# A relational graph layer with a highway gate: node order by one-hot matmuls, the last group's sums kept on chip, x + h kept in the output

## The chip, the cores and the metric

The kernel runs on one core of one Trainium2 chip. The metric is the device time of one execution in microseconds (us). Three timed runs of the kernel before gave 1312.29, 1313.91 and 1315.41 us; their median, 1313.91 us, is the number to be compared. The profile shows one further execution, taken by the hardware profiler.

## What is computed

There are N = 1250 nodes with D = 1024 features, R = 8 relations and E = 20000 edges (src, dst, type), all float32. Cut to what matters, the reference is:

```python
h = relu(layernorm(x))
u = h @ root + bias
for r in range(8):
    sums = segment_sum(h[src] * (type == r), dst)      # a sum over edges
    cnt  = segment_sum(type == r, dst)
    u += (sums / max(cnt, 1)) @ weight[r]
z = concat([u, h]) @ w_gate + b_gate
out = x + tanh(u) * z + h * (1 - z)
```

## The kernel before

**Order of the matrix products.** The kernel multiplies first and sums over edges afterwards: it forms h @ weight[r] for all nodes, and each edge then fetches one row of that product. Eleven matrices are multiplied, one stage each: the eight weights are stages 0 to 7, root is stage 8, the lower half of w_gate (which meets h) is stage 9, called LAST, and the upper half (which meets u) is the gate at the end, stage 10. Every product uses a scheme with seven smaller products in place of eight. Stages 1 to 9 run as seven kinds each, written (stage, kind); `kind` (L284) issues a kind as five calls, numbered 0 to 4, and at each call a hook `between` lets other work be written into the instruction streams. In most kinds the product is split a second time: sums of quarters are made on VectorE (DVE; L264 to L274), TensorE (PE) multiplies (L309), ScalarE (ACT) copies sums in PSUM (L401, L424), and DVE adds in PSUM (L415, L436). PE waits for L401 and L415 inside the kind. In "regular" kinds (L228) the second split is left out. Stage 0 and the gate work in five pairs of node blocks, by `product` (L549, matmuls at L564). There are ten blocks of 128 nodes, the last with 98.

**The order is written out by hand.** Each engine runs its own instructions strictly in the order in which the program writes them. PE, DVE, ACT, GpSimd (POOL) and SyncE (SP) are all scheduled in this way, and a semaphore wait holds back all that stands behind it on its engine. Indirect DMAs (gathers and scatters by a list of row numbers) are issued by POOL, plain ones by SP.

**The index.** Edges are put into a table by destination and group: relations 0 to 4 are group 0, relations 5 to 7 group 1. `to_table` (L813) scatters the 157 columns of edges, 4 bytes each, and follows each scatter with three small memsets on POOL (L823). `order` (L1051) then counts the edges of each node, and ranks the nodes of a group by that count: for each of ten columns a comparison with all 1280 nodes (L838) gives `pos`, the place of each node. `rows_and_weights` (L750) turns places into a list: ten scatters of 128 numbers of 4 bytes to DRAM (L753), one load of the list (L763), `node_key` on POOL (L766), and ten gathers of table rows into `idx` (L705). This is done once per group. `any_over` (L1361) with `largest` (L1343) then asks, by two transposes on PE, whether any node has more edges than the table holds, and `counts` and `weights` make the factors `rcp` and `w_of` in the kinds that follow. At the mark `BEGIN` = (5, 2) the sums over edges may start; one kind ahead of it all engines branch on `n_any` (L1519).

**The sums over edges.** Since nodes are ranked, block d of group g needs at most K[g][d] slots: 118 in group 0, 75 in group 1. A slot (`add_slot`, L1241) is one gather on POOL of 128 rows of 4 KB (L1244) into one of five buffers `got`, and one multiply-add on DVE into the block's sum `u` (L1249). `edges` (L1267) makes a list of steps, one slot each, with the loads and stores of `u` between them, and `spread` (L1302) deals these steps out over the calls of the kinds named to it, by the weights `SHARE`. Group 0 starts its sums from the bias and is dealt over the kinds (5, 2) to (7, 6); its sums are scattered to `u_dram` by node (L711). All engines then branch on `n_pass` (L1568). Group 1 is dealt over the kinds (8, 0) to (9, 5). It starts from gathers of `u_dram` and works blocks 4 to 9 first, then 0 to 3. Blocks 4 to 9 are written to `last_dram` (L1601). To blocks 1 to 3 the product with root is added by an accumulating gather from `hr_dram` (an indirect DMA that adds to what is in its target), to the others by a plain gather into `got` and an addition on DVE (L1608). Sums `u` live in a pool of four buffers.

**The gate.** For each pair i of blocks, seven calls j: `gate_load` brings u of pair i+2 back from `last_dram`; `gate_h` gathers h rows into `got` and takes tanh(u) on ACT (L1683); `gate_turned` transposes u on PE; `gate_less` makes tanh(u) - h on DVE (L1698); `gate_rows` gathers x + h from `xh_dram` and the h part of z by an accumulating gather on top of the bias, multiplies by tanh(u) - h and adds x + h (L1664, L1665). `finish` (L1751) multiplies each quarter of the product by tanh(u) - h and adds the rest, and the finished rows are scattered to `out` (L711). The rows of the last block leave in three pieces (`scatter_piece`, L1636). x + h was written to `xh_dram` by `with_x` (L909) in stages 0 and 1.

Of the kernel before, what the change touches and what calls it, by code (L numbers as in the profile page):

```python
# [21 lines left out]
def tile_rgcn_highway(  # L22
# [53 lines left out]
    BEGIN = (5, 2)  # L76
# [3 lines left out]
    ENDS = 5  # L80
# [36 lines left out]
    xh_dram = dram.tile([N, D], F32, name="xh_dram")  # L117
    last_dram = dram.tile([N, D], F32, name="last_dram")
# [7 lines left out]
    node_dram = [dram.tile([KEYS, 1], I32, name=f"node_dram{g}") for g in range(G)]  # L126
# [567 lines left out]
    pos_i = const.tile([P, G, ND], I32, name="pos_i")  # L694
# [14 lines left out]
    def to_rows(of, frm, at, group):  # L709
        nc.gpsimd.memset(apart, 0.0)  # L710
        ins = nc.gpsimd.indirect_dma_start(  # L711
            out=of, out_offset=bass.IndirectOffsetOnAxis(ap=at, axis=0), in_=frm, in_offset=None)
        tc.declare_no_dep(ins.ins, query=no_wait, group=group, reason="rows differ")
        tc.add_to_no_dep_group(group, ins.ins)
# [35 lines left out]
    def rows_and_weights(g):  # L750

        for d in range(ND):
            ins = nc.gpsimd.indirect_dma_start(  # L753
                out=node_dram[g][:, :],
                out_offset=bass.IndirectOffsetOnAxis(ap=pos_i[:, g, d:d + 1], axis=0),
                in_=ids[:, d:d + 1], in_offset=None,
                bounds_check=KEYS - 1, oob_is_err=False)
            tc.declare_no_dep(ins.ins, query=no_wait, group="nodes", reason="places differ")
            tc.add_to_no_dep_group("nodes", ins.ins)
            if d % 2:  # L760
                yield
        yield
        nc.gpsimd.dma_start(node[:, g, :], node_dram[g].rearrange("(d p) o -> p (d o)", p=P))  # L763
        yield
        yield
        nc.gpsimd.tensor_single_scalar(node_key[:, g, :], node[:, g, :], g * KEYS, op=OP.add)  # L766
        for d in range(ND):
            rows_of(idx[:, g, d, :], table_rows, node_key[:, g, d:d + 1])
            if d % 2:
                yield  # L770
# [42 lines left out]
    def to_table(row_col, at_i, c):  # L813
# [8 lines left out]
        for _ in range(3):  # L822
            nc.gpsimd.memset(apart, 0.0)  # L823
# [17 lines left out]
    room_all = keep.tile([P, 4 * H + 4 * P], F32, name="inner")  # L841
    ys_room = [room_all[:, k * Q:(k + 1) * Q] for k in range(2)]
    with ExitStack() as early:
# [20 lines left out]
        class Normed:  # L864
# [186 lines left out]
        def order():  # L1051

            with tc.tile_pool(name="sort", bufs=1) as sp:
# [16 lines left out]
                for g in range(G):  # L1070
# [4 lines left out]
                    nc.vector.tensor_copy(pos_i[:, g, :], pos[:, g * ND:(g + 1) * ND])  # L1075
                    for _ in rows_and_weights(g):
                        pass
                for _ in range(3):
                    yield
# [132 lines left out]
    with ExitStack() as edges_part:  # L1212
# [40 lines left out]
        def new_u(d):  # L1253

            return upool.tile([P, D], F32, name="u")

        def first_u(g, d):

            n = nrows(d)
            u = new_u(d)  # L1260
# [6 lines left out]
        def edges(g, blocks, to, late=0, more={}):  # L1267
# [4 lines left out]
            nb = len(blocks)  # L1272
            starts = [late + sum(K[g][d] for d in blocks[:b]) for b in range(nb + 1)]
            leaves = [starts[b + 1] - 1 + GOT for b in range(nb)]
            reads = [max(-1, starts[b] - (9 if d in more else 5),
                         leaves[b - UB] if b >= UB else -1) for b, d in enumerate(blocks)]
            u, then = {}, {}
            for t in range(-1, leaves[-1] + 4):
                for b, d in enumerate(blocks):
                    if starts[b] <= t < starts[b + 1]:  # L1280
                        k = t - starts[b]
                        add_slot(u[d], g, d, k, idx[:, g], w_of[:, g])
                for b, d in enumerate(blocks):
                    if t == leaves[b]:
# [3 lines left out]
                for b, d in enumerate(blocks):  # L1288
                    if t == reads[b]:
                        u[d] = first_u(g, d)  # L1290
                    if d in more and t == starts[b] - 4:
# [10 lines left out]
        def spread(e, total, of):  # L1302

            share = [0 if s == LAST and n > ENDS else SHARE[n] for s, n in of]
            parts, said = CALLS * sum(share), [0, 0]

            def between(k):
                s, n, _ = at_call
                said[0] += 0 if s == LAST and n > ENDS else SHARE[n]
# [3 lines left out]
                if said[0] == parts:  # L1313
# [5 lines left out]
        def kinds(s, n, last):  # L1319

            return [(a, b) for a in range(s, last + 1) for b in range(7) if (a, b) >= (s, n)]
# [21 lines left out]
        def largest(*pairs):  # L1343
            p = sum_bank("ps_q")
            for k, (of, to) in enumerate(pairs):
                nc.tensor.transpose(p[:1, k * P:(k + 1) * P], of, ident)
            for k, (of, to) in enumerate(pairs):
                nc.vector.reduce_max(to, p[:1, k * P:(k + 1) * P], axis=AX.X)
        def whole(of, to, add, least):

            nc.vector.tensor_scalar(of, of, float(add), float(least), op0=OP.add, op1=OP.max)
            nc.vector.tensor_copy(to, of)

        def passes_over(*more):

            top = const.tile([1, 1], F32, name="top")
            largest((most[:, 0:1], top), *more)
            whole(top, n_over, MORE - SLOTS, 0.0)
            nc.vector.tensor_single_scalar(n_over, n_over, 2, op=OP.arith_shift_right)

        def any_over():  # L1361

            bad = const.tile([1, 1], F32, name="bad")
            passes_over((most[:, 2:3], bad))
            whole(bad, n_far, 0.0, 0.0)
            nc.vector.tensor_max(n_any, n_over, n_far)
        def beside(e, total, s, i, last):


            between = spread(e, total, kinds(s, i, last))  # L1370
            while s <= last:
                step(s, i, between)
                s, i = next(steps, (NM, 0))
# [7 lines left out]
        def beside_group():  # L1381

            yield
            while at_call[2] != 2:
                yield
            any_over()
            yield
            for g in range(G):
                yield from counts(g)
                yield  # L1390
# [94 lines left out]
        def order_again():  # L1485
# [13 lines left out]
            for g in range(G):  # L1499
# [8 lines left out]
                nc.vector.tensor_copy(pos_i[:, g, :], pos[:, g * ND:(g + 1) * ND])  # L1508
                for _ in rows_and_weights(g):
# [49 lines left out]
        first_group = with_ready(edges(0, range(ND), u_back(0), LATE))  # L1559
        next(first_group)  # L1560
        s, i = beside(first_group, sum(K[0]) + LATE + 1, s, i, R0[2] - 1)
# [35 lines left out]
        HELD = 4  # L1597

        def to_last(d, u):
            n = nrows(d)  # L1600
            nc.sync.dma_start(last_dram[d * P:d * P + n, :], u[:n])  # L1601
# [231 lines left out]
```

## Time and profile before

| | |
|---|---|
| median of three timed runs | 1313.91 us |
| the profiled execution | 1306.43 us |
| its span, first to last instruction | 1304.5 us |
| PE busy | 1266.7 us of the span |
| DVE busy | 978.2 us |
| POOL busy | 629.5 us |
| ACT busy | 252.1 us |
| DMA moved | 286.25 MB |
| slots, gather and multiply-add (L1244, L1249) | 193 |

How to read it: the profile is of one execution. Rows named by a source line group the instructions that this line issued. "Idle before, releaser" says how long the engine stood still ahead of an instruction and what ended that wait; "issue" means that the profile shows nothing the engine waited for, "remote" that a semaphore moved and no instruction in the profile is seen to have moved it. A view by windows gives the busy time of each engine in a stretch of the span, with the granted TensorE clock (1.00 is full speed), the mean busy share of the 16 DMA engines, and GB/s.

### The profile page before, as it was taken

The numbers are of one execution on the slowest core, as the hardware profiler recorded it, in microseconds if no ns is written. First come the engines' busy times: TensorE is split into PE (matmuls) and PEld (weight loads), VectorE is DVE, ScalarE is ACT, GpSimd is POOL, SyncE is SP. The second block draws the span as 40 slices with busy tenths as digits, with TensorE's granted clock in tenths as the row PEclk, the third lists the DMA queues.
The fourth block names the chain that finished last, engine by engine and source line by source line (L and its number), as shares of the span: only waits on it lengthen the run. The fifth ranks groups of instructions, "written<-read, shape, count | busy, mean of one in ns | idle before, by whom it ended". The sixth has DMA issues, their size and how long they took to land. (4 is left out here: it accounts for less than half of the span.)

```text
span 1304.5 us, 13959 instructions
## 1 busy us (share of the span) xinstructions
PE 1266.7 (97%) x4430; PEld 832.6 (64%) x4430; DVE 978.2 (75%) x1377; ACT 252.1 (19%) x462; POOL 629.5 (48%) x975
## 2 busy tenths in 40 slices
PE   9999999999999999799999999999899998999996
PEld 5444777777777777575767666675656655644443
DVE  7963576555454896666899999997889897757974
ACT  3452221221121121112102111210110021102210
POOL 0046666665663045411356665665376557305531
PEclk9999999999999999899999999999999998999999
DMA  8777244534634746453757989799589868949951
GB/s 307 249 222 196 94 154 155 205 126 145 211 118 149 245 98 151 110 191 106 244 189 245 324 305 383 269 330 339 183 308 341 331 193 264 315 153 287 324 158 61
DMA packets 126597, 286.25 MB, mean 219 GB/s; under 512 B 33733, under 2 KB 35362, under 8 KB 126386
## 3 DMA queue, kind: packets, MB, share of 16 engines
q1 hardware_dynamic: 81890, 164.96, 37.6%
q0 software_dynamic: 44336, 119.80, 28.7%
q8 instruction: 35, 0.57, 0.2%
q10 hardware_dynamic: 288, 0.52, 0.1%
q14 instruction: 48, 0.39, 0.1%
HBM read 217.52 MB, written 82.71 MB: 230 GB/s over the span
## 5 line engine op out<-in xcount | busy, mean ns | idle before, releaser
L309 PE MATMUL ps<-w,h_all 128*128 128x256 f32 (+1 forms) x1216 | 371.7, 454 | 9.0 <-issue 9.0
L1244 POOL DMA_INDIRECT got<-y,idx x193 | 262.2, 1359 | 233.5 <-DVE u L1249 134.3
L309 PEld LDWEIGHTS ps<-w,h_all 128*128 128x128 f32 x1216 | 231.9, 191 | 128.9 <-issue 105.3
L1249 DVE SCALAR_TENSOR_TENSOR u<-got,w_of,u 128x1024 f32<-128x1024 f32 (+1 forms) x193 | 247.1, 1283 | 34.3 <-DMA got<-y,idx 25.9
L815 POOL DMA_INDIRECT table<-row_col,at_i x157 | 166.1, 1058 | 171.3 <-issue 100.5
L316 PE MATMUL ps_b<-w,h_all 128*128 128x512 f32 x504 | 226.6, 592 | 0.6 <-PEq L1519 0.6
L309 PE MATMUL ps_n<-w,w 128*128 128x256 f32 x800 | 192.2, 383 | 13.1 <-DVE ps L415 11.2
L309 PEld LDWEIGHTS ps_n<-w,w 128*128 128x128 f32 x800 | 151.8, 191 | 59.3 <-DVE ps L415 17.8
L316 PEld LDWEIGHTS ps_b<-w,h_all 128*128 128x128 f32 x504 | 95.8, 190 | 94.8 <-issue 91.6
L564 PE MATMUL ps_b<-w,h_all 128*128 128x512 f32 x312 | 139.3, 593 | 1.0 <-ACT row L614 0.7
L564 PEld LDWEIGHTS ps_b<-w,h_all 128*128 128x128 f32 x312 | 58.6, 190 | 73.6 <-issue 70.1
L415 DVE TENSOR_TENSOR ps<-ps_n,inner 128x256 f32<-128x256 f32 x100 | 40.8, 428 | 80.4 <-PE ps L309 75.5
L309 PE MATMUL ps<-w,w 128*128 128x256 f32 x400 | 94.8, 380 | 0.0
L309 PE MATMUL ps_q<-w,w 128*128 128x256 f32 x400 | 94.6, 379 | 0.2 <-DMA w<-lefts_dram 0.2
L309 PE MATMUL ps_n<-w,h_all 128*128 128x256 f32 x400 | 94.5, 379 | 0.0
L424 ACT COPY ps<-ps_n 128x512 f32<-128x512 f32 x100 | 53.0, 574 | 193.9 <-PE ps_n L309 182.6
L401 ACT COPY ps<-ps_n 128x256 f32<-128x256 f32 x100 | 32.2, 360 | 280.9 <-PE ps_n L309 216.8
L309 PEld LDWEIGHTS ps_n<-w,h_all 128*128 128x128 f32 x400 | 76.1, 190 | 15.5 <-issue 5.7
L309 PEld LDWEIGHTS ps<-w,w 128*128 128x128 f32 x400 | 76.4, 191 | 10.5
L309 PEld LDWEIGHTS ps_q<-w,w 128*128 128x128 f32 x400 | 75.9, 190 | 11.0 <-DVE w L367 0.6
L224 DVE TENSOR_TENSOR w<-w,w 128x2048 f32<-128x2048 f32 x36 | 82.2, 2284 | 0.3
L823 POOL MEMSET apart<- 128x1 f32 x471 | 52.2, 111 | 18.1
(213 smaller groups left out, 1195.2 us busy)
## 6 DMA issues: line engine op xcount, KB each, us to landing
w<-in_L_gnn_weight_dram SPq DMA_DIRECT2D x31, 1024.0 KB
w<-lefts_dram SPq DMA_DIRECT2D x48, 512.0 KB
y<-row SPq DMA_DIRECT2D x84, 256.0 KB
y<-w SPq DMA_DIRECT2D x42, 256.0 KB
w<-in_L_gnn_w_gate_dram SPq DMA_DIRECT2D x8, 1024.0 KB
lefts_dram<-w SPq DMA_DIRECT2D x14, 512.0 KB
h_dram<-h_all SPq DMA_DIRECT2D x9, 512.0 KB
y<-row SPq DMA_DIRECT2D x9, 512.0 KB
```

The costliest lines, as they stand in the source:

```text
L224: nc.vector.tensor_sub(w[to], w[a], w[b])
L309: nc.tensor.matmul(p, a[:, k], b[:, k], start=(fresh and k == 0), stop=(k == a.shape[1] - 1), skip_group_check=True)
L316: nc.tensor.matmul(to, h_op[NP - 1][:, ORDER[n], k], w[:, k], start=(fresh and k == 0), stop=(k == KQ - 1), skip_group_check=True)
L401: nc.scalar.copy(banks[2 * u][:, :H], xs[u])
L415: nc.vector.tensor_add(banks[2 * u][:, H:], xs[u], ys[:, u * H:(u + 1) * H])
L424: nc.scalar.copy(banks[2 * u + 1].rearrange("p (a n) -> p a n", a=2), xs[u][:, None, :].to_broadcast([P, 2, H]))
L564: nc.tensor.matmul(b[:, at], aop[:, i, k, :], w.of[i][:, k, at], start=(fresh and k == 0), stop=(k == KQ - 1), skip_group_check=True)
L815: ins = nc.gpsimd.indirect_dma_start(out=table[:, :], out_offset=bass.IndirectOffsetOnAxis(ap=at_i[:, c:c + 1], axis=0), in_=row_col[:, c: ...
L823: nc.gpsimd.memset(apart, 0.0)
L1244: nc.gpsimd.indirect_dma_start(out=t[:n], out_offset=None, in_=y[g][:, :], in_offset=bass.IndirectOffsetOnAxis(ap=at[:n, d, k:k + 1], axis=0),
L1249: nc.vector.scalar_tensor_tensor(u[:n], t[:n], w, u[:n], op0=OP.mult, op1=OP.add)
```

## The change

1. **Node order** (`nodes_in_order` in place of `rows_and_weights`). The place of each node is split into its high part and its low 7 bits. DVE makes two one-hot tables from them (128 x 1280 and 128 x 200, bf16), ten matmuls of 128 x 20 on PE invert the order into a bank of PSUM, and DVE forms `node` and `node_key` from it. The matmuls stand at call 2 of a kind. The twenty scatters L753, the two loads L763 and `node_dram` are gone; the gathers of `idx` stay. `any_over` is moved from the kind after the index up to stage 1, between the scatters of edges.
2. **Where the sums stand.** `BEGIN` is (5, 1). Group 0 is dealt over (5, 1) to (8, 2) and its branch on `n_pass` stands ahead of (8, 3). Group 1 is dealt over (8, 3) to (9, 6) and, with the weight `GATE` = 6, over the first three pairs of the gate. Its blocks run in the order 0 to 9.
3. **The last group's sums stay on chip.** `last_dram`, its stores and `gate_load` are gone. The sums of blocks 4 to 8 lie in `h_all`, in the places of the first two left factors, which kinds (9, 0) and (9, 1) read last. The product with root is added by an accumulating gather for all ten blocks: for blocks 3 to 9 four steps ahead of their first slot, for blocks 0 to 2 after their last, from call 3 of (9, 0) on.
4. **The gate.** `with_x` stores x + h to `out`, and `xh_dram` is gone. tanh is taken of -u, and h is added to it by an accumulating gather. The h part of z is gathered one pair ahead. `finish` adds z to the product and then multiplies by -1 and by h - tanh(u), and the rows are added to `out` by accumulating scatters. `got` is no longer used for rows of hr, h and x + h.

```diff
-    BEGIN = (5, 2)
+    BEGIN = (5, 1)
+    CHANGE = (8, 3)
-    ENDS = 5
+    GATE = 6
+    U_LATER = range(4, 9)
+    HR_LATER = 3
...
-    def rows_and_weights(g):
-        for d in range(ND):
-            ins = nc.gpsimd.indirect_dma_start(
-                out=node_dram[g][:, :],
-                out_offset=bass.IndirectOffsetOnAxis(ap=pos_i[:, g, d:d + 1], axis=0),
-                in_=ids[:, d:d + 1], in_offset=None,
-                bounds_check=KEYS - 1, oob_is_err=False)
...
-        nc.gpsimd.dma_start(node[:, g, :], node_dram[g].rearrange("(d p) o -> p (d o)", p=P))
...
-        nc.gpsimd.tensor_single_scalar(node_key[:, g, :], node[:, g, :], g * KEYS, op=OP.add)
+    def nodes_in_order(g, pos, ids_f, a, b, small, now=False):
...
+        nc.vector.tensor_copy(hi_i, pos)
+        nc.vector.tensor_single_scalar(hi_i, hi_i, 7, op=OP.arith_shift_right)
+        nc.vector.tensor_copy(hi, hi_i)
+        nc.vector.scalar_tensor_tensor(lo, hi_i, float(-P), pos, op0=OP.mult, op1=OP.add)
+        nc.vector.tensor_tensor(a, lo[:, :, None].to_broadcast([P, ND, P]),
+                                many[:, None, :].to_broadcast([P, ND, P]), op=OP.is_equal)
+        nc.vector.tensor_tensor(b[:, :, :ND], hi[:, :, None].to_broadcast([P, ND, ND]),
+                                many[:, None, :ND].to_broadcast([P, ND, ND]), op=OP.is_equal)
+        nc.vector.tensor_tensor(b[:, :, ND:], b[:, :, :ND],
+                                block[:, :, None].to_broadcast([P, ND, ND]), op=OP.mult)
+        nc.vector.tensor_scalar(b[:, :, :ND], b[:, :, :ND], ids_f[:, :1], None, op0=OP.mult)
+        yield
+        while not now and at_call[2] != 2:
+            yield
+        p = sum_bank("ps_q")
+        for c in range(ND):
+            nc.tensor.matmul(p[:, :2 * ND], a[:, c], b[:, c], start=(c == 0), stop=(c == ND - 1))
+        nc.vector.tensor_copy(lo_f := small[:, P + 4 * ND:P + 5 * ND], p[:, :ND])
+        nc.vector.scalar_tensor_tensor(node[:, g, :], p[:, ND:2 * ND], float(P), lo_f,
+                                       op0=OP.mult, op1=OP.add)
+        nc.vector.tensor_single_scalar(node_key[:, g, :], node[:, g, :], g * KEYS, op=OP.add)
...
-                nc.sync.dma_start(xh_dram[self.d * P:self.d * P + n, :], to[:n])
+                nc.sync.dma_start(out[self.d * P:self.d * P + n, :], to[:n])
...
+            checks = [any_over]
             for c in range(NCH):
                 to_table(row_col, at_i, c)
                 if c % 3:
                     yield
+                    if checks and at_call[0] and at_call[2] == 2:
+                        checks.pop()()
...
+            if g == G - 1 and d in U_LATER:
+                return h_op[d - U_LATER[0]][:, :2].rearrange("p a k f -> p (a k f)")
             return upool.tile([P, D], F32, name="u")
...
-        s, i = beside(first_group, sum(K[0]) + LATE + 1, s, i, R0[2] - 1)
+        s, i = beside(first_group, sum(K[0]) + LATE + 1, s, i, CHANGE)
...
-            t = got()
-            rows_of(t[:n], hr_dram[:, :], node[:n, LG, d:d + 1])
-            us[d] = u
-            return lambda: nc.vector.tensor_add(u[:n], u[:n], t[:n])
+            rows_of(u[:n], hr_dram[:, :], node[:n, LG, d:d + 1], OP.add)
...
-                to_rows(out, t[:n], node[:n, LG, d:d + 1], "out")
+                to_rows(out, t[:n], node[:n, LG, d:d + 1], "out", OP.add)
...
-                hs[part] = got()
-                rows_of(hs[part][:n], h_dram[:, :], node[:n, LG, d:d + 1])
-                nc.scalar.activation(place_of("d", i, part)[:n], us[d][:n], AF.Tanh)
+                nc.scalar.activation(place_of("d", i, part)[:n], us[d][:n], AF.Tanh, scale=-1.0)
...
-                nc.vector.tensor_sub(dt[:n], dt[:n], hs[part][:n])
+                rows_of(place_of("d", i, part)[:n], h_dram[:, :], node[:n, LG, d:d + 1], OP.add)
...
-        between = spread(last, LATE + sum(K[LG]) + GOT + 4, kinds(s, i, LAST))
+        last = edges(LG, keep_u, LATE, {d: add_hr for d in range(HR_LATER, ND)}, 4, False)
+        between = spread(last, LATE + sum(K[LG]) + 8, kinds((s, i), (NM - 1, NP - 2)))
...
-                    nc.vector.tensor_mul(to, of[:n], place_of("d", i, part)[:n, at])
-                    nc.vector.tensor_add(to, to, place_of("z", i, part)[:n, at])
+                    nc.vector.tensor_add(to, of[:n], place_of("z", i, part)[:n, at])
...
+                    nc.vector.scalar_tensor_tensor(to, to, -1.0, place_of("d", i, part)[:n, at],
+                                                   op0=OP.mult, op1=OP.mult)
```

More of the change, by code (lines that the diff above doesn't have):

```diff
@@ L1074, in order @@
                         yield
[L1075 to L1079, printed above, removed]
+                    yield from nodes_in_order(g, pos[:, g * ND:(g + 1) * ND], ids_f, junk,
+                                              sp.tile([P, 2 * ND * ND], BF16, name="b"),
+                                              sp.tile([P, P + 5 * ND], F32, name="small"))
         HEAVY = True
@@ L1287, in edges @@
                     then[t]()
[L1288 to L1289 removed]
+                for d in blocks:
+                    if t == reads[d]:
                         u[d] = first_u(g, d)
[L1291 removed]
+                    if d in more and t == starts[d] - 4:
                         more[d](d, u[d])
@@ L1341, in passes_needed, with beside @@
             nc.vector.tensor_max(n_pass, n_over, beyond_i)
[L1343 to L1371, printed above, removed]
+        def beside(e, total, s, i, end):
+            between = spread(e, total, kinds((s, i), end))
+            while (s, i) != end:
                 step(s, i, between)
-                s, i = next(steps, (NM, 0))
+                s, i = next(steps)
             return s, i
```

194 lines of the change are left out of this document (92 added, 102 removed).

## The prediction

> **What bounds the kernel now.** I read the page first, then who PE waited for, then the engines by windows of 25 us, and the timeline where PE stood still.
>
> ```profile
> span 1304.5 us, 13959 instructions
> PE 1266.7 (97%) x4430; PEld 832.6 (64%) x4430; DVE 978.2 (75%) x1377; ACT 252.1 (19%) x462; POOL 629.5 (48%) x975
> PE ps_n L309 <- DVE ps L415: 11.2, 5, 5.6
> PE ps L309 <- issue: 9.0, 1, 9.0
> PE ps_n L309 <- ACT ps L401: 1.8, 4, 1.1
> PE ps_b L564 <- ACT row L614: 0.7, 1, 0.7
> ```
>
> PE is busy for 1266.7 of 1304.5 us, so 37.8 us are all that an edit can win on PE, and any instruction added to PE costs its length. The waits (total, times, longest, in us) name the stalls: 9.0 us once, with a releaser that the profile does not know, and 11.2 + 1.8 us where PE waited for DVE or, through ACT, mostly for DVE again. The windows show where. Columns: busy us and count of PE, PEld, DVE, ACT and POOL, then granted clock, DMA share and GB/s.
>
> ```profile
> 525.00:550.00 25.00, 18.23 (x69) 14.32 (x70) 12.98 (x29) 3.34 (x7) 8.59 (x10) 0.86 0.43 94
> 875.00:900.00 25.00, 23.93 (x78) 14.39 (x77) 24.83 (x35) 2.28 (x5) 12.69 (x13) 1.00 0.94 326
> 900.00:925.00 25.00, 22.59 (x83) 15.24 (x82) 18.08 (x23) 2.87 (x6) 9.69 (x9) 1.00 0.80 286
> 925.00:950.00 25.00, 23.69 (x82) 15.18 (x81) 17.88 (x25) 5.69 (x11) 13.83 (x10) 1.00 0.62 188
> 950.00:975.00 25.00, 23.60 (x81) 14.99 (x80) 22.13 (x22) 4.62 (x9) 17.61 (x13) 1.00 0.93 333
> 1000.00:1025.00 25.00, 25.00 (x73) 13.55 (x72) 24.54 (x30) 1.06 (x2) 15.73 (x12) 1.00 0.97 352
> 1075.00:1100.00 25.00, 19.45 (x68) 14.10 (x67) 19.97 (x20) 3.18 (x7) 19.22 (x14) 0.86 0.83 253
> 1200.00:1225.00 25.00, 25.00 (x71) 11.96 (x70) 24.45 (x30) 4.99 (x8) 16.54 (x15) 1.00 1.04 326
> 1275.00:1300.00 25.00, 19.15 (x52) 9.42 (x51) 14.36 (x20) 1.75 (x3) 4.38 (x7) 0.99 0.11 40
> ```
>
> Three places lose time: the node order near 530, the slots' stages from 875 to 975 and at 1090 (DVE at 24 of 25 us there), and the tail after PE's last matmul. In the gate PE loses nothing (25.00 of 25) though DVE is at 24 and DMA is full. So DVE work taken out of the gate wins nothing by itself.
>
> **Part 1, node order.** Timeline rows (start, length, instruction, [idle before]):
>
> ```profile
> 181.73 0.98 POOL L815 DMA_INDIRECT table<-row_col,at_i  x1 [0.63 <-issue]
> 183.76 1.14 POOL L815 DMA_INDIRECT table<-row_col,at_i  x1 [0.63 <-issue]
> 516.62 1.03 POOL L753 DMA_INDIRECT node_dram<-ids,pos_i  x1 [0.30 <-issue]
> ...
> 528.79 0.98 POOL L753 DMA_INDIRECT node_dram<-ids,pos_i  x1 [0.30 <-issue]
> 531.15 1.06 ACT L424 COPY ps<-ps_n 128x512 f32<-128x512 f32 x2 [10.10 <-remote]
> 531.77 3.58 PE L309 MATMUL ps<-w,h_all 128*128 128x256 f32 x8 [8.96 <-issue]
> 535.18 1.89 PE L309 MATMUL ps_n<-w,h_all 128*128 128x256 f32 x8
> ```
>
> From 516.62 to 529.77 POOL issues the ten 4-byte scatters of group 1, one each (528.79 - 516.62)/9 = 1.35 us, and directly after the last ACT, PE and DVE go on. The scatters of edges have the same shape but stand 2.03 us apart (three memsets between), and PE has no such stall among all 157. I take the dense scatters as the cause; the change removes them. Won: 8.96 us, and the half clock after it, 3.58 - 1.89 = 1.69; together **10.65**.
>
> Added on PE: 20 pairs of weight load and 20-column matmul.
>
> ```profile
> L135 PEld LDWEIGHTS <-ident x5: 98/98/105, 1.4 to 136.3; 128*128 128x128 bf16 x5
> L1346 PE MATMUL ps_q<-ident,most x3: 272/272/273, 519.0 to 802.7; 128*1 128x128 f32 x3
> L783 DVE TENSOR_TENSOR more<-codes 128x2512 bf16<-128x2512 int16 x3 | 4.4, 1474 | 0.1
> L1249 DVE SCALAR_TENSOR_TENSOR u<-got,w_of,u 128x1024 f32<-128x1024 f32 (+1 forms) x193 | 247.1, 1283 | 34.3 <-DMA got<-y,idx 25.9 <-DMA u<-in_L_gnn_bias_dram 6.0
> ```
>
> The trace has no 20-column matmul. Below, a pair can't be shorter than the bf16 load, 0.098; above, 0.098 + 0.272. The load is the nearer row: I take 0.13, so 20 x 0.13 = 2.6 (2.0 to 7.4). On DVE, ahead of the matmuls: one comparison of 1280 elements, 1280/2512 of 1.474 = 0.75, and eight small operations, by estimate 0.2 each: 2.3 us per group, where DVE is the engine that PE waits for next (the matmul, then L401 behind L352 and L355). One of the ranking comparisons per kind moves later, which gives some of it back; I put 1.5 for both groups, bounds 0 and 2 x 2.3. Sum **4.1** lost (2.0 to 12.0). Queued behind the one-hot's wait on PE is the kind's own next product. What POOL no longer does lies on no path of PE: the counts come a kind later. `any_over` costs its two transposes wherever it stands: 0.
>
> **Part 2, dealing the slots.** Group 0 has 118 + 5 = 123 steps, before over 19 kinds (6.5 each), now over 23 (5.35). DVE saves 1.12 x 1.283 = 1.4 us per kind of about 15.5, 9%, in a stage where it was full. PE's idle time in 875 to 950 is 1.07 + 2.41 + 1.31 = 4.8. The last 1.31 stands around the branch between the groups, which only moves; I keep it and win **3.5** (0 to 4.8). The three kinds of stage 8 that now carry group 0 bring nothing to SP but the stores that stood there.
>
> Group 1:
>
> ```profile
> 1050.62 2.19 POOL L705 DMA_INDIRECT u<-hr_dram,node  x1 [6.26 <-DMA hr_dram<-w]
> 1073.82 1.75 POOL L1244 DMA_INDIRECT got<-y,idx  x1 [3.46 <-DVE u L1249]
> 1079.98 1.28 DVE L1249 SCALAR_TENSOR_TENSOR u<-got,w_of,u 128x1024 f32<-128x1024 f32 x1 [3.63 <-DMA got<-y,idx]
> 1087.44 1.22 DVE L1608 TENSOR_TENSOR u<-u,got 128x1024 f32<-128x1024 f32 x1
> 1090.59 3.78 PE L309 MATMUL ps_n<-w,w 128*128 128x256 f32 x8 [5.55 <-DVE ps L415]
> 1094.16 2.21 PE L309 MATMUL ps<-w,w 128*128 128x256 f32 x8
> ```
>
> POOL waited for a free `got`, the next gather landed late, DVE stood 3.63 us, made up by L1608, and reached L415 5.55 us late. With the half clock (3.78 - 1.89 and 2.21 - 1.89) that cost 7.76; with the 1.40 in 950 to 975, 9.2. Now 87 steps go over 11 kinds and the gate. By the weights, 555 of 681 parts lie in the kinds: 6.4 steps each in place of 6.8, 0.4 x 1.283 = 0.5 us of DVE less, and none of the five `got` is lent to hr, h or x + h rows. Against it stand more waits of POOL (the second rival). I take half, **4.5** won; the ends are all of it, 9.2, and minus two more such stalls, -15.5. The first wait for hr (6.26) stays, one call later.
>
> **Parts 3 and 4, gate and tail.** By step 71 of 87 the gate begins, so 8 slots are left: 8 x 1.28 = 10 us of DVE over three pairs, against 37 operations like L1608 of 1.22 us that go (L1608 seven times, L1664, L1665 and L1698 ten times each by the code), 36 of them in the gate. Cover: no PE gap; if it were gone, a pair would cost its DVE excess, and there is none. The accumulating forms:
>
> ```profile
> L705 POOL DMA_INDIRECT h_all<-z_dram,node x6 | 9.6, 1604 | 1.8 <-issue 1.8
> L705 POOL DMA_INDIRECT got<-h_dram,node x10 | 10.8, 1084 | 16.1 <-DVE u L1608 11.3 <-DVE u L1249 2.5 <-issue 1.8
> 1257.00:1261.00 4.00, 4.00 (x23) 2.60 (x22) 2.89 (x6) 1.14 (x3) 0.14 (x2) 1.00 1.00 220
> 1273.00:1275.00 2.00, 2.00 (x6) 0.94 (x5) 0.00 (x0) 0.58 (x1) 0.39 (x2) 1.00 0.95 391
> ```
>
> In the first window mostly accumulating gathers of z move, 220 GB/s at share 1.00; in the second plain scatters of `out`, 391 at 0.95. So a block of 0.52 MB holds the 16 DMA engines 2.4 us when accumulated and 1.3 when plain. 27 more accumulates (7 hr, 10 h, 10 out) are 65 us; the 49 blocks that go (7 hr, 10 h, 10 x + h, 10 out, 12 to and from `last_dram`) were 64. Even: 0.
>
> The tail is open to view:
>
> ```profile
> 1291.21 3.62 PE L564 MATMUL ps<-w,h_all 128*128 128x256 f32 x16
> 1293.72 0.97 POOL L711 DMA_INDIRECT out_dram<-row,node  x1 [1.38 <-DVE row L1761]
> 1294.99 0.97 POOL L711 DMA_INDIRECT out_dram<-row,piece_at  x1 [0.19 <-issue]
> 1296.27 0.97 POOL L711 DMA_INDIRECT out_dram<-row,piece_at  x1 [0.19 <-issue]
> ```
>
> Three scatters leave back to back after 1293.72, and the span ends 7.3 us after the last. An accumulate occupies POOL 1.60 in place of 0.97: 3 x 0.63 = 1.9; its data 0.6 more by the doubled time for the last pieces: **2.5** lost (1.9 to 8, should a read of DRAM ahead of each write not be overlapped). The Trainium skill (DMA: Bandwidth & Descriptors, "Anatomy of one DMA") says a semaphore fires only when the last byte is confirmed in its target, DRAM being the slowest; an accumulate reads that target first. With its access latency of 0.2 to 2 us ("Latency and other measured facts") in place of my 0.6, the time would be 1301.5 to 1303.3, an estimate. No row before shows an accumulate into DRAM.
>
> **The sum.** 10.65 - 4.1 + 3.5 + 4.5 - 2.5 = 12.05. The profiled execution took 1306.43, so it would take 1294.4. The median of the runs shown is 7.48 higher; I carry that over: 1313.91 - 12.05 = **1301.9**.
>
> **Rivals.**
> (a) The stall at 530 isn't from the scatters. For it: "issue" and "remote" name no cause; the waits show only one such stall, though group 0 had ten such scatters too; `largest` stood in the same kind. Against: a third use of `largest` near 800 shows no gap. Then 10.65 is not won: 1312.6.
> (b) Slower: POOL loses its lead. u of blocks 4 to 8 now lies where PE reads until (9, 1), and the h gather waits for tanh; whatever gather stands behind such a wait on POOL starts late, DVE waits for it, L415 behind it, PE last, as at 1090. It decides from two such stalls in the ten kinds: 2 x 7.76, and the 4.5 not won: 1301.9 + 20.0 = 1321.9. For it: the 6.26 wait above; against: PE is through the first left factor's block early in (9, 1).
> (c) DVE's relief changes nothing (3.5 + 4.5 lost): 1309.9.
> (d) All of 9.2 + 4.8 is won, one-hot 2.6 and tail 1.9: 1301.9 - 4.7 - 1.3 - 1.5 - 0.6 = 1293.8.
>
> **How the numbers follow.** Forecast 0.48, (a) 0.17, (b) 0.14, (c) 0.12, (d) 0.09. A measurement here tells about 0.2%, 2.6 us: faster is below 1311.3, slower above 1316.5. Faster: 0.48 + 0.09 + 0.09 of (c) + 0.05 of (a) = 0.71; within: 0.12 + 0.03 = 0.15; slower 0.14. The range 1293.5 to 1313.5 holds all cases but (b) and the edges.
>
> **What would show it.** Right: no PE gap over 3 us between 500 and 560, clock 1.00 there; the ten matmuls of each group within 1.5 us; PE's wait for L415 under 6 us in all; L711 near 1.6 us, and the span ending about 12 us after PE's last matmul (9.7 before). Wrong: a gap near 520 without L753 (a); POOL waiting for PE or ACT ahead of L1249's gathers, with new halves of the clock after 985 (b); gaps of PE in the gate.

## The result and the profile after

The changed kernel takes 1301.97 us (median of four runs, 1300.81 to 1302.13) against 1313.85 for the kernel before: a ratio of 0.9908, with a 95% interval of 0.9891 to 0.9925. The forecast was 1301.9. The number agrees and the working behind it does not, as the views below show: one part won 11 us more than forecast, another lost 15 us where no loss was forecast, and the two nearly cancel.

The page of the changed kernel (span, then busy time, share and instructions of each engine):

```profile
span 1300.1 us, 13912 instructions
PE 1267.6 (98%) x4450; PEld 833.0 (64%) x4450; DVE 941.5 (72%) x1360; ACT 251.5 (19%) x462; POOL 610.5 (47%) x943
```

Who PE waited for in the changed kernel (us in total, times, longest; waits of the first 70 us and some short ones left out):

```profile
PE ps_n L564 <- DVE h_all L546: 6.6, 1, 6.6
PE ps_b L564 <- ACT row L587: 4.0, 2, 3.0
PE ps_n L309 <- DVE ps L415: 2.2, 1, 2.2
PE ps_q L508 <- DVE h_all L513: 1.6, 1, 1.6
PE ps_q L309 <- DVEq L1539: 1.4, 1, 1.4
PE ps_b L564 <- DVE w L192: 1.3, 1, 1.3
PE ps_n L309 <- ACT ps L401: 0.3, 1, 0.3
```

The 9.0 us without a releaser are gone, and of 11.2 + 1.8 us behind L415 and L401 2.5 are left. In their place stand waits of lines 564, 508, 546 and 587, which belong to the gate, where PE had waited for nothing but 0.7 us. The windows of the changed kernel (columns as in the prediction) say when:

```profile
525.00:550.00 25.00, 25.00 (x108) 20.13 (x107) 18.67 (x39) 3.50 (x8) 7.74 (x8) 1.00 0.63 196
900.00:925.00 25.00, 25.00 (x102) 19.00 (x101) 22.23 (x28) 4.92 (x11) 10.76 (x9) 1.00 0.94 337
925.00:950.00 25.00, 25.00 (x78) 14.50 (x77) 20.85 (x22) 5.64 (x11) 14.29 (x10) 1.00 0.54 173
1075.00:1100.00 25.00, 25.00 (x78) 14.50 (x77) 19.96 (x25) 1.80 (x4) 17.32 (x14) 1.00 0.97 298
1200.00:1225.00 25.00, 15.71 (x30) 6.67 (x31) 14.97 (x21) 3.68 (x6) 11.93 (x12) 0.86 0.87 189
```

Of the stalls that the prediction named, those up to 1050 are gone, and of the one at 1090 a smaller one is left near 1071 (2.2 us behind L415). From 1200 to 1225 PE works 15.71 us where it had worked all 25, at clock 0.86, while DVE is busy for only 15 us and DMA, at share 0.87, moves 189 GB/s where it had moved 326. So the gate waits for data. The chain of one such wait, from the timeline of the changed kernel (start, length, instruction, [idle before]):

```profile
1158.10 2.58 POOL L1287 DMA_INDIRECT got<-y,idx  x1 [0.30 <-issue]
1170.96 1.55 POOL L704 DMA_INDIRECT h_all<-z_dram,node  x1 [10.27 <-DMA z_dram<-w]
1174.67 2.01 POOL L704 DMA_INDIRECT w<-h_dram,node  x1 [0.30 <-issue]
1178.82 1.03 POOL L1287 DMA_INDIRECT got<-y,idx  x1 [0.30 <-issue]
1186.48 1.30 DVE L1292 SCALAR_TENSOR_TENSOR h_all<-got,w_of,h_all 128x1024 f32<-128x1024 f32 x1 [10.01 <-DMA got<-y,idx]
1193.49 1.28 DVE L1292 SCALAR_TENSOR_TENSOR h_all<-got,w_of,h_all 128x1024 f32<-128x1024 f32 x1 [5.11 <-DMA got<-y,idx]
1198.79 1.06 ACT L1689 ACTIVATE h_all<-h_all 128x1024 f32<-128x1024 f32 x1 [10.54 <-DVE row L1751]
1199.05 1.63 POOL L715 DMA_INDIRECT out_dram<-row,node  x1 [11.38 <-DVE row L1751]
1202.04 0.59 ACT L587 COPY row<-ps_b 128x512 f32<-128x512 f32 x1
1202.68 7.13 PE L564 MATMUL ps_b<-w,h_all 128*128 128x512 f32 x16 [3.00 <-ACT row L587]
1203.03 1.09 POOL L1287 DMA_INDIRECT got<-y,idx  x1 [0.30 <-issue]
1211.04 1.28 DVE L1292 SCALAR_TENSOR_TENSOR u<-got,w_of,u 98x1024 f32<-98x1024 f32 x1 [8.44 <-DMA got<-y,idx]
1216.42 6.20 PE L564 MATMUL ps_n<-w,h_all 128*128 128x512 f32 x8 [6.61 <-DVE h_all L546]
1288.53 3.62 PE L564 MATMUL ps<-w,h_all 128*128 128x256 f32 x16
```

The gather of a slot is issued at 1178.82, 20.7 us after that of the slot before it (1158.10). In between POOL stood 10.27 us at the first gather of z, by the profile in wait for the store of `z_dram`, and then issued four accumulating gathers (two of z, two of h). The slot's data are there at 1186.48, 7.7 us after the issue; the median over all 193 gathers of slots in this execution is 6.4 us, so the larger part of the delay lies ahead of the issue. DVE waits for the slots in order (10.01, then 5.11), finishes its rows late, so that tanh on ACT starts late, and the copy L587 behind tanh holds PE. At 1211 it happens again, without ACT: the gather of 1203.03 stands on POOL behind two scatters of rows, for the first of which POOL had waited 11.38 us for DVE, and its data come 8.0 us after the issue. PE's last matmul ends at 1292.15; the span ends 7.9 us later, where before it ended 9.7 after PE.

### The profile page after: what moved, and what is told of

The parts are those of the page before. It is cut to its first block, busy times and chain, and to the rows that moved or that the text cites. A ratio compares the mean times of both kernels' runs of the same rounds, so it can differ in the third digit from the quotient of the medians.

```text
span 1300.1 us, 13912 instructions
## 1 busy us (share of the span) xinstructions
PE 1267.6 (98%) x4450; PEld 833.0 (64%) x4450; DVE 941.5 (72%) x1360; ACT 251.5 (19%) x462; POOL 610.5 (47%) x943
## 4 chain that ended last, share of the span: by engine, by line
PE 37%; issue 8%; DMA 5%; POOL 4%; DVE 1%; POOLq 0%; DVEq 0%
PE ps L309 19%; PE ps_n L309 8%; PE ps_b L316 8%; DMA got<-y,idx 4%; PE ps_q L309 3%; POOL out_dram L715 1%; POOL h_all L704 1%; POOL got L1287 1%; POOL w L704 1%; DVE u L1292 1%; DMA z_dram<-w 0%; POOL u L704 0%; DVE h_all L1292 0%; DVE w L367 0%; DVE ps L436 0%
## 5 line engine op out<-in xcount | busy, mean ns | idle before, releaser
L1287 POOL DMA_INDIRECT got<-y,idx x193 | 258.8, 1341 | 286.0 <-DVE u L1292 183.1
L833 POOL DMA_INDIRECT table<-row_col,at_i x157 | 170.6, 1086 | 171.7 <-issue 100.4
L1292 DVE SCALAR_TENSOR_TENSOR u<-got,w_of,u 128x1024 f32<-128x1024 f32 (+1 forms) x166 | 212.6, 1282 | 26.8 <-DMA got<-y,idx 24.7
L316 PE MATMUL ps_b<-w,h_all 128*128 128x512 f32 x504 | 226.7, 592 | 0.0
L316 PEld LDWEIGHTS ps_b<-w,h_all 128*128 128x128 f32 x504 | 95.7, 190 | 94.3 <-issue 90.9
L564 PE MATMUL ps_b<-w,h_all 128*128 128x512 f32 x312 | 139.8, 594 | 7.3 <-ACT row L587 4.0
L564 PEld LDWEIGHTS ps_b<-w,h_all 128*128 128x128 f32 x312 | 58.3, 190 | 81.4 <-issue 68.9
L415 DVE TENSOR_TENSOR ps<-ps_n,inner 128x256 f32<-128x256 f32 x100 | 42.2, 431 | 91.4 <-PE ps L309 91.0
L401 ACT COPY ps<-ps_n 128x256 f32<-128x256 f32 x100 | 32.0, 360 | 275.7 <-PE ps_n L309 260.4
L309 PEld LDWEIGHTS ps_q<-w,w 128*128 128x128 f32 x400 | 75.9, 190 | 12.2 <-issue 1.8
L704 POOL DMA_INDIRECT idx<-table,node_key x20 | 24.6, 1228 | 77.4 <-DVE node_key L786 71.9
```

What stands on the lines that cost most here:

```text
L309: nc.tensor.matmul(p, a[:, k], b[:, k], start=(fresh and k == 0), stop=(k == a.shape[1] - 1), skip_group_check=True)
L316: nc.tensor.matmul(to, h_op[NP - 1][:, ORDER[n], k], w[:, k], start=(fresh and k == 0), stop=(k == KQ - 1), skip_group_check=True)
L401: nc.scalar.copy(banks[2 * u][:, :H], xs[u])
L415: nc.vector.tensor_add(banks[2 * u][:, H:], xs[u], ys[:, u * H:(u + 1) * H])
L564: nc.tensor.matmul(b[:, at], aop[:, i, k, :], w.of[i][:, k, at], start=(fresh and k == 0), stop=(k == KQ - 1), skip_group_check=True)
L704: nc.gpsimd.indirect_dma_start(out=to, out_offset=None, in_=of, in_offset=bass.IndirectOffsetOnAxis(ap=at, axis=0), compute_op=op)
```

## The experiments

Before each: its edit and what was expected. Ratios are to the kernel before on the same chip.

**1. The kernel before again**, unchanged.

> The kernel before once more, unchanged. Its timed runs (1312.3 to 1315.4) are 7.5 us over its one profiled execution (1306.43), while those of the changed kernel agree with its profile (1302.13). If the profile of before was an execution that happened to lack a stall, this profile shows about 1313 and names 6 to 8 us of idle time of PE that the first one lacks. If timing simply adds 7 us to a profiled execution of this kernel, this profile shows 1306 again, with the same gaps of PE.

Measured: 1315.68 (ratio 0.9997, 0.9984 to 1.001); the profiled execution took 1314.72. The sixty timed runs of before in this study lie between 1307.23 and 1324.11, so the execution that the prediction read, at 1306.43, was faster than every one of them. PE's waits in this second execution, then its timeline:

```profile
PE ps_n L309 <- DVE ps L415: 21.9, 5, 13.0
PE ps_q L309 <- DMA w<-lefts_dram: 3.5, 2, 3.3
```

```profile
531.50 0.98 POOL L753 DMA_INDIRECT node_dram<-ids,pos_i  x1 [0.30 <-issue]
546.67 1.02 POOL L763 DMA_DIRECT2D node<-node_dram  x1 [14.20 <-issue]
553.72 0.25 POOL L766 TENSOR_SCALAR node_key<-node 128x10 int32<-128x10 int32 x1 [6.02 <-DMA node<-node_dram]
565.81 0.95 POOL L705 DMA_INDIRECT idx<-table,node_key  x1 [0.30 <-DMA idx<-table,node_key]
568.20 0.31 DVE L742 TENSOR_SCALAR got<-idx 128x280 f32<-128x280 int32 x1 [21.49 <-DMA idx<-table,node_key]
569.71 0.80 PE L309 MATMUL ps_n<-w,w 128*128 128x256 f32 x1 [12.96 <-DVE ps L415]
```

There is no stall during the scatters here. Instead the chain behind them is long: the last scatter at 531.5, the load 14.2 us later, its data after 6 more, ten gathers of `idx` up to 566.8. The counts of group 1 (L742) stand on DVE in wait for the last of these, 21.49 us, and L415, for which PE waits, stands behind them. What the load waited for in its 14.2 us, the profile does not show. The wait of 3.3 us for a left factor (`lefts_dram`) follows directly behind the scatters and is absent in experiment 3. So the node order cost 3.3 + 13.0 us of PE in this execution, and 9.0 in the one of the prediction, each with half clock behind it.

**2. The scatters spaced.** After each scatter of nodes, three memsets:

```diff
             tc.add_to_no_dep_group("nodes", ins.ins)
+            for _ in range(3):
+                nc.gpsimd.memset(apart, 0.0)
```

> Before, with three small memsets on POOL after each of the twenty scatters of nodes, so that they stand as far apart as the scatters of edges (2.0 us for 1.35). Theory (ten scatters back to back hold PE up at 530): the gap of 9.0 us and the half clock behind it go, about 1303 against a median of 1313.9, less up to 7 us if the later index delays what follows. Rival (something else in that kind holds PE up): the gap near 530 stays, at 1313 or somewhat above.

Measured: 1316.83 (1.0012, 0.9994 to 1.0031). Nothing is won. In its profile the chain ends when it did in experiment 1 (the last gather of `idx` at 566.3, there 566.8); PE reached its wait behind L415 some 4.5 us earlier, and so stood there longer:

```profile
PE ps_n L309 <- DVE ps L415: 24.1, 4, 16.9
```

**3. One-hot node order alone**: `nodes_in_order` of the change in the kernel before, in place of `rows_and_weights`; `any_over`, the dealing, the gate and the output stay.

> Before, with the node order by one-hot matmuls alone (any_over, the dealing of the slots, the gate and the output as before). Theory: the stall near 530 is won and the matmuls cost 4 of it: 10.65 - 4.1 = 6.5 faster, 1307. If the rest of the change brings the gain: 1313 or slower. If the scatters cost more than the one gap in the timed runs: below 1304.

Measured: 1297.07 (0.9861, 0.9843 to 0.9879), 18 us faster, and faster than the whole change. PE's waits that are left:

```profile
PE ps_n L309 <- DVE ps L415: 11.0, 4, 5.8
PE ps_n L309 <- ACT ps L401: 3.1, 5, 1.1
PE ps_q L777 <- DVE b L771: 0.4, 1, 0.4
```

The one-hot costs PE 0.4 us of waiting for its tables. The other two rows are the slots' stages, as before, but for 0.84 us behind L401 at 450, where DVE is still at the ranking. `any_over` with `largest` stands here where it stood before, and the stall is gone. So one part of the change brings 18 us, and the rest of it takes about 6 away (0.9908 against 0.9861).

**4. Slots behind the finishing of rows.** In the gate's hook `between(j)` is moved from ahead of `gate_rows` to the end.

> After, with the slots of each call of the gate written behind the finishing of rows and the tanh of that call, not ahead of them. Theory (the slots of the gate stand on DVE in wait for late gathers, ahead of the finishing of rows, and so hold up tanh on ACT and at last PE at 1202 and 1216): most of the 9.6 us of these two gaps goes, about 1294. Rival (the transfers are late because the DMA engines are full between 1100 and 1250, whatever the order): the gaps only move, 1300 to 1304.

Measured: 1302.29 (0.989, 0.9872 to 0.9909). The time is the rival's: the two gaps are now 5.4 us each (both ps_n L564 <- DVE L546). But the edit moves the slots' gathers on POOL along with their work on DVE. POOL still stands 12.2 us at the gather of z and 13.7 at the scatter of rows, with slots behind both. So this run does not separate the order on DVE from that on POOL, and the rival's "whatever the order" does not survive experiments 10 to 12.

**5. No slots in the gate.**

```diff
         def add_slot(u, g, d, k, at, w):
+            if at_call[0] == NM - 1:
+                return
```

> After, with the slots that are dealt to the gate left out (neither their gather nor their multiply-add is done; the edges in them are missing from the sums). Theory (in the gate each slot's gather lands behind the accumulating gathers of z and h, which hold the DMA engines twice as long, and DVE, which waits for it in order, keeps the left factors and the finishing of rows back): the gaps of PE at 1203 and 1216 (9.6 us) and the half clock behind them go, 1289 to 1292. Rival (the accumulating transfers alone make PE wait): the gaps stay, 1300 to 1302.

Measured: 1285.52 (0.9795, 0.9766 to 0.9824): the eight slots of the gate cost 15 us, 1.13% of the time. The waits of PE for L546, L587 and L513 in the gate are gone, though POOL waits 14.2 us ahead of the first gather of z here too: with no slot behind it, that wait costs PE nothing.

**6. and 7. Plain transfers** in place of accumulating ones: the ten gathers of h in `gate_d`, and all scatters to `out`.

```diff
-                rows_of(place_of("d", i, part)[:n], h_dram[:, :], node[:n, LG, d:d + 1], OP.add)
+                rows_of(place_of("d", i, part)[:n], h_dram[:, :], node[:n, LG, d:d + 1])
```

```diff
-                to_rows(out, t[:n], node[:n, LG, d:d + 1], "out", OP.add)
+                to_rows(out, t[:n], node[:n, LG, d:d + 1], "out")
```

> After, with the gathers of h on top of tanh as plain gathers (h in place of h - tanh(u): the tanh is lost). Ten transfers of 0.5 MB then hold the DMA engines 1.3 us each in place of 2.4. Theory (the slots' gathers stand behind the accumulating ones): each slot lands 2 us earlier per pair, the two gaps of 9.6 us shrink to some 5, 1296 to 1299. Rival (order on DVE alone): 1300 to 1302.

> After, with plain scatters of the rows to the output (the sum with x + h is lost). The prediction put 2.5 us on the accumulating scatters at the end: 1299.5 by that. The traces speak against it: the last accumulating scatter was followed by the end of the span 5.8 us after it began, the last plain one of before by 8.2 us. By them this is 1302 to 1304. In the gate the scatters stand ahead of the slots' gathers of pair 2 as well, which could win some of the 9.6 us: 1298.

Measured: 1300.76 (0.9906, 0.9877 to 0.9934) with plain gathers of h, no different from the changed kernel, so that the gathers of h accumulate is not what delays the slots; 1295.59 (0.9866, 0.9838 to 0.9895) with plain scatters. In the second, PE's last row and the scatters' group (count, busy, mean ns) are:

```profile
1285.37 3.62 PE L564 MATMUL ps<-w,h_all 128*128 128x256 f32 x16
```

```profile
L715 POOL DMA_INDIRECT out_dram<-row,piece_at x3 | 3.1, 1024 | 19.2 <-DVE row L1751 19.0 <-issue 0.2
```

Its span is 1294.8, so it ends 5.8 us after PE, against 7.9 with the accumulating scatters: these cost 2.1 at the end, though I expected the contrary from the comparison with before. The rest of the gain lies in the gate, where the wait for L546 shrank from 6.6 to 2.0 us, while those for L587 grew from 4.0 to 5.8.

**8. One-hot alone, begun one kind earlier**: `BEGIN = (5, 1)` in the kernel of experiment 3.

> Before with the one-hot node order, and the sums begun one kind earlier, at (5, 1), so that group 0 is dealt over 20 kinds in place of 19: 6.15 steps each for 6.47. Theory (DVE's relief lets PE run through the stages 5 to 7): the gaps of PE between 850 and 925 (1.11 + 0.56 + 0.91 + 0.35 + 0.98 in the run with one-hot alone, 3.9 us) shrink by half or more, 1294 to 1296 against 1297.1. Rival (the gaps come from the order of the steps around the stage's change, not from their density): 1297.

Measured: 1300.48 (0.9904, 0.988 to 0.9929), 3 us slower than experiment 3 (by the ratios, since the two ran on different chips, 5 to 6). Its profile shows no gap of PE over 0.3 us between 600 and 960, so the relief of DVE is real. What it wins is lost at the branch on `n_any`:

```profile
573.80 0.91 DVE L1236 MEMSET got<- 128x1024 f32 x1 [0.20 <-issue]
581.57 1.29 DVE L367 TENSOR_TENSOR w<-w,ps 128x512 f32<-128x512 f32 x2 [3.80 <-DVEq L1532]
581.52 3.75 PE L309 MATMUL ps_q<-w,w 128*128 128x256 f32 x8 [6.04 <-DVEq L1532]
```

DVE stands 3.8 us at the branch (3.6 in experiment 3, 3.4 in the changed kernel). At (5, 0) the next product is split, so PE soon needs DVE: 6.0 us lost here, with counts still ahead of the branch on DVE, and 1.4 in the changed kernel. In experiment 3 the branch stands ahead of the regular kind (5, 1), whose first product (L316, 3.7 us) needs nothing of DVE.

**9. Counts later.** In the kernel before, eight calls go by ahead of the counts of group 1:

```diff
             for g in range(G):
+                if g == G - 1:
+                    for _ in range(8):
+                        yield
                 yield from counts(g)
```

> Before, with the counts of group 1 (the first reading of its index on DVE) eight calls later, some 25 us; the scatters of nodes and all else stay. Theory (in the ordinary run of before the chain of scatters, load and gathers ends at 568, DVE waits for it in order, and PE waits for DVE 13 us): the 13 us and the half clock behind them go, about 15 us faster, 1297 to 1301, and the 3.1 us that the last drain of POOL lost with the one-hot order stay. Rival (the scatters hold PE up directly, or fill the DMA engines so that its left factor is late): at most the wait for the index moves, 1308 to 1313.

Measured: 1307.73 (0.9958, 0.9939 to 0.9978), between the two. The wait behind L415 at 569 is gone, but the profiled execution has the stall of the prediction's profile again, and longer:

```profile
522.40 1.89 PE L309 MATMUL ps<-w,w 128*128 128x256 f32 x8
536.19 1.06 ACT L424 COPY ps<-ps_n 128x512 f32<-128x512 f32 x2 [10.06 <-remote]
536.81 3.77 PE L309 MATMUL ps<-w,h_all 128*128 128x256 f32 x8 [12.53 <-ACT ps L424]
```

So the order by scatters and load has two prices: a stall while the scatters are issued, in two of the four profiles that have them, and the late index, in the other two. In the first profile, where the stall had held PE up first, DVE waited 4.0 us for the index, at 560, and PE 0.9 behind it. The one-hot order ends both. Why the stall comes in some executions only, and which semaphore is late, the profile does not show ("remote"); it stays open.

**10. to 12. The slots of the gate moved up.** In 10 they are dealt over the first pair alone; 11 adds `BEGIN = (5, 2)`; 12 is 10 with the gather of z for the first pair one call later, which on POOL moves one gather, that of the last slot, from behind the two gathers of z to ahead of them.

```diff
-    GATE = 6
+    GATE = 18
...
-        between = spread(last, LATE + sum(K[LG]) + 8, kinds((s, i), (NM - 1, NP - 2)))
+        between = spread(last, LATE + sum(K[LG]) + 8, kinds((s, i), (NM - 1, 1)))
...
-            if i == 0 and j == 2:
+            if i == 0 and j == 3:
                 gate_z(0)
```

> After, with the eight slots of the gate dealt over the first pair alone (weight 18 over seven calls for 6 over twenty-one), so that nearly all their gathers are issued ahead of the accumulating gather of z, for which POOL waits 10 us at 1171. Theory (what hurts is the place behind the accumulating gathers, not the work of the slots): the gaps at 1203 and 1216 go, less some new wait for DVE in the first pair, which also makes the sums of the weight factors: 1288 to 1294. Rival (eight slots in the gate cost their 16 us wherever they stand, as leaving them out won): 1300 to 1304.

> As the run with the slots in the first pair, and the sums begin at (5, 2) again, so that the branch on n_any stands a kind later. The branch cost PE 0.45 + 1.40 us at 574 in the changed kernel, 0.45 + 6.04 where it was moved alone, and nothing over 0.3 in the run with one-hot alone. Theory: 1.5 us of these come back, while group 0 goes over 22 kinds for 23 (5.6 steps for 5.35) at no cost: 1 to 2 us under the run with the slots in the first pair. Rival (the denser group 0 brings its gaps back): 1 to 3 us over it.

> As the run with the slots in the first pair, with the accumulating gather of z for that pair one call later (call 3 for call 2). On POOL this moves one gather alone: that of the last slot now stands ahead of the two transfers of z in place of behind them. Theory (a slot behind accumulating gathers lands late, and DVE passes the delay on): DVE's wait of 3.32 us at 1183 goes, and with it 3 of the 4.74 us that PE lost at 1186, and some of the half clock: 1292 to 1295 against 1297.2. Rival (z then comes late for the finishing of rows of the first pair, and the loss moves on): 1297 or slower.

Measured: 1297.23 (0.9888, 0.9866 to 0.9911) for 10, 1302.72 (0.9918, 0.9899 to 0.9937) for 11, 1290.46 (0.9816, 0.979 to 0.9841) for 12. By its ratio, 10 is not clear of the changed kernel (0.9908). Run 12 is the fastest kernel of the study that computes everything: 24 us under before, and within 3 us of experiment 5, which leaves the eight slots out (0.9795). So it is the place of the slots that cost most of the 15 us, and not their work. Timeline of 10, then of 12:

```profile
1173.17 1.71 POOL L704 DMA_INDIRECT h_all<-z_dram,node  x1 [0.30 <-issue]
1175.19 1.65 POOL L1287 DMA_INDIRECT got<-y,idx  x1 [0.30 <-issue]
1183.01 1.28 DVE L1292 SCALAR_TENSOR_TENSOR u<-got,w_of,u 98x1024 f32<-98x1024 f32 x1 [3.32 <-DMA got<-y,idx]
1186.34 4.11 PE L564 MATMUL ps_n<-w,h_all 128*128 128x512 f32 x5 [4.74 <-DVE h_all L546]
```

```profile
1167.22 1.57 POOL L1287 DMA_INDIRECT got<-y,idx  x1 [0.30 <-issue]
1169.84 1.57 POOL L704 DMA_INDIRECT h_all<-z_dram,node  x1 [1.05 <-issue]
1177.21 1.32 DVE L1292 SCALAR_TENSOR_TENSOR u<-got,w_of,u 98x1024 f32<-98x1024 f32 x1
1180.57 1.98 PE L564 MATMUL ps_n<-w,h_all 128*128 128x512 f32 x4 [2.14 <-DVE h_all L546]
```

The wait of 3.32 us is gone, PE's gap shrinks by 2.6, and the half clock behind it goes too (five matmuls took 4.11 us, now four take 1.98). The gather of the last slot is issued 8.0 us earlier, at 1167.22 for 1175.19. That it also lands faster after its issue is not shown: 7.8 us in 10, and at most 10.0 in 12, where DVE took it without waiting. In 11 the branch cost PE nothing over 0.3 us, as hoped, but a gap came, with half clock behind it:

```profile
990.29 3.68 PE L309 MATMUL ps_n<-w,w 128*128 128x256 f32 x8 [3.96 <-DVE ps L415]
```

It does not lie in the denser group 0, where PE has no gap, but behind the branch between the groups: the first gather of `u` for group 1 is issued at 970.22 (967.34 in 10), and DVE stands 6.93 us there for its first slot (3.10 in 10). Neither expectation names this, and why that gather is later is not shown.

## Why the prediction was right in number and wrong in its working

**Part 1, the stall (10.65).** The step "I take the dense scatters as the cause; the change removes them" was half right. That the one-hot order wins it is shown (experiment 3), and that a stall comes while the scatters are issued is seen twice (the first profile and 9), never without them. But setting them further apart wins nothing (2; whether it spares the stall the runs do not tell, since that comes in some executions only), and the larger price was one that the profiled execution did not show: the late index (1). By the forecast's terms part 1 was worth 10.65 - 4.1 = 6.6 us; alone it won 18. Rival (a) is refuted by experiment 3, where `largest` keeps its place and the stall is gone.

**The base.** "The median of the runs shown is 7.48 higher; I carry that over" was the wrong step: the difference was no constant, but in good part the very cost that the change removes. It was a sign, in plain view, that the profiled execution was not the ordinary one.

**The one-hot's price (4.1).** Too high. One 20-column matmul takes 0.17 us and one load 0.096, but ten pairs in a row took 0.40: "a pair can't be shorter than the bf16 load, 0.098" was wrong, since in a row they overlap. PE's wait for the tables was 0.4 in experiment 3. About 1.2 us, 0.8 of them matmuls.

**Part 2 (3.5 + 4.5).** Right in kind, small in size. ("DVE at 24 of 25 us there" holds for 875 to 900 alone; where most of the gaps lay, 900 to 975 and 1075 to 1100, the windows have it at 18 to 22.) PE's waits behind L415 and L401 fell from 13.0 us in the first profile to 2.5, the gaps from 875 to 975 to nothing, and the stall at 1090 to one of 2.2 at 1071. The 1.31 us that I left with "the branch between the groups, which only moves" went too. The other branch, on `n_any`, I did not cost at all; it took PE 1.4 + 0.4 us, for 0.6 in the kernel before, so 1.2 more.

**Parts 3 and 4, the gate (0).** This is the step that failed: "Cover: no PE gap; if it were gone, a pair would cost its DVE excess, and there is none." I looked for DVE's load, which fell, and not for when its data come. The eight slots cost 15 us (experiment 5), since their gathers stand on POOL behind instructions that wait (10.27 us for z, 11.38 for rows) and are issued late, and DVE waits in order. That it is their place, experiments 10 and 12 show, which moved them ahead and had 12 of the 15 back. How much the transfers issued ahead of a slot add after its issue stays open: it landed in 7.7 and 8.0 us for a median of 6.4, and plain gathers of h changed nothing (6). The prediction's own sign of being wrong came, "gaps of PE in the gate". "27 more accumulates [...] Even: 0" compared bytes and engine time over the kernel; the accumulates came together between 1050 and 1225, where slots now stood behind them. Rival (b) had this mechanism (a gather that stands behind a wait on POOL and starts late, DVE, PE) with the wrong place: not in the ten kinds but in the gate.

**The tail (-2.5).** The price of the accumulating scatters was nearly right: 2.1 for 2.5 (experiment 7), of which 1.4 are on POOL, where I had 1.9, and 0.8 behind it, where I had 0.6. The Trainium skill's access latency (DMA: Bandwidth & Descriptors, "Latency and other measured facts") in place of my 0.6 would have made 2.1 to 3.9 of it, an estimate; the traces put it at the low end. Yet the tail became shorter, 7.9 for 9.7, for a reason that I did not see, told below.

In sum: 18 won for 6.6 in part 1 (7 to 8 of the difference is the base that I carried over, and 3.1 of the 18 lie in the tail), about 10 for 8 in part 2, 2 lost for 2.5 by the accumulating scatters, 15 lost in the gate where I had put 0, and 1 at a branch that I did not cost. That adds up to some 10 us for the 12 measured; the pieces come from different runs, each uncertain by 2 to 4 us. The forecast of 12 came out because the errors cancel: that is luck.

## What to carry to other kernels

When the profiled execution and the timed runs differ by more than the effect, take a second profile before any sum; the difference may be the very thing. Ask of a step that is moved not only what its engine has free, but what its gather will stand behind on the queue that issues it: one gather moved ahead of two others, and so issued 8 us earlier, was worth 7 us by the medians (9 by the ratios, since the two ran on different chips). And take a change of many parts apart: one part of this one brought 18 us, and the rest gave 6 of them back until the order on one queue was mended (24 us in experiment 12).

## What the runs showed that was not expected

The span's end depends on the node order. In experiment 3, whose tail is that of before, plain scatters included, PE's last matmul is this:

```profile
1283.92 3.62 PE L564 MATMUL ps<-w,h_all 128*128 128x256 f32 x16
```

It ends at 1287.54 and the span at 1294.1, 6.6 us later; in experiment 8 it is 6.6 too, and in the kernel before it is 9.7, in both of its profiles and in experiments 2 and 9. So the node order by scatters and load, 750 us earlier, lengthens the end by 3.1 us. What the program waits for there is not shown. The other thing is the branch: in experiments 3 and 8 and in the changed kernel DVE stands 3.4 to 3.8 us where all engines branch on `n_any`, and PE pays 0.3 us there, 6.5 or 1.9, by the kind that stands behind it.
